# A graph layer on one core: other pacing of edge sums beside the residual loop, mixed rows three chunks ahead

## The chip, the core and the metric

The kernel runs on one core of a Trainium2 chip. A core has five engines, each with a program and a queue of its own: PE (matrix products and transposes, with weight loads shown as PEld), DVE (vector work), ACT (activations, copies, and issue of DMAs), POOL (elementwise work, and issue of gathers, that is, DMAs whose row numbers come from memory) and SP (issue of DMAs). 16 DMA engines carry all transfers. An engine works its instructions strictly in the order in which the program has them; one that waits for a semaphore holds up all behind it. The metric is the time of one execution in device microseconds (us), less is better. A measured time of a kernel here is the median of a few runs.

## What is computed

A layer of a graph transformer over 10,000 nodes with 512 features and 160,000 weighted edges, all in float32. Cut to what matters:

```
xn  = layernorm(x)
# graph part: messages along edges, summed at the edge's target (dst is sorted)
agg = segment_sum((xn @ W)[src] * edge_weight, dst);   gnn = relu(agg + bias)
# mixing part: attention that is linear in the nodes
q, k, v = heads(xn @ w_qkv.T);  q = softmax(q over 64 features);  k = softmax(k over nodes)
context = k.T @ v  (per head);  mix = layernorm(context applied to q, @ w_out.T) * gamma
x1  = x + gnn + mix
# feed-forward part: experts with weights chosen from the mean of layernorm(x1)
out = x1 + experts(layernorm(x1))
```

## The kernel before

**Tiling.** Rows are handled in 20 chunks: 19 of 512 nodes (128 partitions with four nodes each, SUB = 4) and a last one of 272. Features are four blocks of 128 (KB = 4). A product of 128 rows by 512 columns is four matmul calls in the source; the trace shows two passes for each, so "x8" in its rows is one such product.

**Edges.** `xn_d` holds the normalized rows in device memory. The edges stand in 1250 tiles of 128 edges. For each tile POOL gathers 128 rows of `xn_d` into a buffer `msg` (L556, 24 buffers in the pool `edge_m`, L826), DVE makes a selector `sel` of 128 x 32 (L562, L564), and PE multiplies (L574, the product `pm`): four tiles side by side fill the 128 output rows, one window of 32 rows each. Such a group of four tiles (eight up to tile 768, where two tiles share a window) is copied by ACT (L577, `part`) and written to `part_d` in device memory (L578). Where a target node's edges run over from one window to the next, the overlap is added by a carry: a DMA on POOL's queue that adds rows of `part_d` to others (L641). The matrix W is applied later, to the sums.

**The stages.** First rows are normalized and keys and queries are made (up to about 1070 us): queries are written to `qT_d`, and G gathers keys times rows. Then a data-dependent branch (L676 to L684, not taken here), then the small products that make the mixing matrix `mix` from G (L906 to L932). Then the residual loop (L1011 to L1063) makes x1 for each chunk, and the last stage (L1308 to L1332) applies the experts.

**The residual loop.** `attention(c)` (L986) loads the queries of a chunk (`qT`, one buffer) and its rows (`xt`, one buffer) on SP's queue, makes four products `po` with `mix`, and lets ACT and DVE turn them into `ot` (four buffers). It runs two chunks ahead of the loop: chunks 0 and 1 ahead of it (L1011), chunk c + 2 in round c. In round c the summed messages of the chunk's nodes, gathered by POOL from `part_d` into `at` (L963, two buffers, 1 MiB a chunk), are turned by 16 transposes into `aT` (`transposed`, L192, all copies on ACT), multiplied by `wg` (four products `pg`, L200) and added to `ot`, which SP writes to `x1_d` (L1032). The transposes and the next chunk's gather (`nodes_rows`, L1016) stand just ahead of the last of the four `po` products (L994).

**What sets the order.** PE's order is written out by hand (L903, `manual_schedule`): PE executes in the order of the Python calls. The order on the other engines is set by the compiler's scheduler from the same program. Edge groups are strewn among PE's other products by `work` (L664): each call reports estimated own work of PE in us (0.83 for each 128 x 512 matmul call, `PRODUCT`), the total is kept in `done[1]`, and edges are consumed up to tile `done[1] / PACE`, with PACE = 0.9. `edges_to` (L654) issues the gathers of a group when more than 16 tiles (AHEAD) are no longer in hand, so POOL's program runs 16 to 20 tiles ahead of PE's. A chunk's node gather may read only sums that are complete. The table AT_HAND (L35) says up to which window that must be for chunks below a number, and `far_enough` (L945) consumes all edges up to there, wherever PE's order stands, before the gather is issued:

```
for n, w in AT_HAND:
    if c < n:
        edges_to(min(NQ, past(w // GROUP, LAG + LEAD) + 1))
        return w * WIN
```

For the last two chunks it consumes all edges, adds the last carry, and the 17 DMAs that load the experts' weights (`experts_weights`, L284) follow on POOL's queue.

Of the kernel before, what the change touches and what calls it, by code (L numbers as in the profile page):

```python
# [9 lines left out]
F32 = mybir.dt.float32  # L10
# [20 lines left out]
KEPT = 2  # L31
PRODUCT = 0.83
PACE = 0.9

AT_HAND = [(5, 320), (7, 384), (8, 424), (9, 472), (10, 520), (11, 560), (12, 604), (13, 640), (14, 680), (15, 716), (16, 752),  # L35
           (17, 788), (18, 820)]
# [14 lines left out]
def gps_layer_kernel(  # L51
# [230 lines left out]
    held_w = {}  # L282

    def experts_weights():  # L284
        wp = held_w["pool"] = ctx.enter_context(tc.tile_pool(name="f_w", bufs=1, reuse_waits="tile"))
        w1_sb = held_w["w1"] = wp.tile([P, KB, NBASE * P], F32, name="w1_sb")
        w2_sb = held_w["w2"] = wp.tile([P, NBASE, D], F32, name="w2_sb")
        held_w["w1_sum"] = wp.tile([P, 4, KH, PAIRS * P], F32, name="w1_sum")
        b1_sb = held_w["b1"] = wp.tile([P, NF], F32, name="b1_sb")
        b2_sb = held_w["b2"] = wp.tile([NE, D], F32, name="b2_sb")  # L290
        held_w["b2_rows"] = wp.tile([P, D], F32, name="b2_b")
        rw_sb = held_w["router"] = wp.tile([P, KB, NP], F32, name="rw_sb")
        nc.scalar.dma_start(rw_sb, router_t.rearrange("(k p) d -> p k d", p=P))
        nc.scalar.dma_start(b1_sb[:, : NF - 1], b1_a)
        nc.scalar.dma_start(b1_sb[: fsz[-1], NF - 1 :], b1_b)
        nc.scalar.dma_start(b2_sb, b2)
        for j in range(KB):
            for g in range(P // SQ):
                nc.gpsimd.dma_start(w1_sb[g * SQ : (g + 1) * SQ, j, :], features(w1)[j, g, :, : NBASE * P])
        nc.gpsimd.dma_start(w2_sb, w2[: NBASE * P, :].rearrange("(f p) d -> p f d", p=P))  # L300
# [81 lines left out]
    with ExitStack() as ph:  # L382
# [266 lines left out]
            carried.append((past(end // GROUP, LAG), partial(carry, w, end)))  # L649

        done = [0, 0.0]
        EARLY_TOTAL = PRODUCT * KB * EARLY * 3 * KB

        def edges_to(stop):  # L654
# [9 lines left out]
        def work(us):  # L664

            done[1] += us
            if not pools:

                normal_rows(int(done[1] / EARLY_TOTAL * (NCH + 1)) + 2 - len(normal))
                return  # L670
            edges_to(groups_of(int(done[1] / PACE)))

        in_order = ph.enter_context(ExitStack())
        in_order.enter_context(tc.manual_schedule(engines={mybir.EngineType.PE}))
# [231 lines left out]
        with ExitStack() as pb:  # L906
            tmp = pb.enter_context(tc.tile_pool(name="c_tmp", bufs=1, side="right", reuse_waits="tile"))
            rk = small.tile([P, KB], F32, name="rk")
            nc.vector.reciprocal(rk, ksum)
            GT = tmp.tile([P, KB, D], F32, name="GT")  # L910
            transposed(GT, G, P, psum, "ps")
            edges_to(done[0] + 1)
            heads = tmp.tile([P, KB, P], F32, name="heads")
            nc.vector.memset(heads, 0.0)
            for cb in range(KB):
                pc = psum.tile([P, P], F32, name="pctx", tag="ps")
                for kb in range(KB):
                    nc.tensor.matmul(pc, GT[:, kb, cb * P : (cb + 1) * P],
                                     wv[:, kb, cb * P : (cb + 1) * P],
                                     start=kb == 0, stop=kb == KB - 1)  # L920
                for b in (0, HEAD):
                    blk = slice(b, b + HEAD)
                    nc.vector.tensor_scalar(heads[blk, cb, blk], pc[blk, blk],
                                            rk[blk, cb : cb + 1], QSCALE, op0=ALU.mult, op1=ALU.mult)
                edges_to(done[0] + 1)
                pt = psum.tile([P, P], F32, name="pht", tag="ps")
                nc.tensor.transpose(pt, heads[:, cb, :], ident)
                headsT = tmp.tile([P, P], F32, name="headsT", bufs=2)
                nc.vector.tensor_copy(headsT, pt)
                pm = psum.tile([P, D], F32, name="pmix", tag="ps")  # L930
                nc.tensor.matmul(pm, headsT, wo[:, cb, :], start=True, stop=True)
                nc.scalar.copy(mix[:, cb, :], pm)  # L932
        kv_ctx.close()

        done[1] = max(done[1], tiles_of(done[0])[0] * PACE)

# [20 lines left out]
        def gathered(c):  # L959
            r = chunks[c][1]  # L960
            n_rows = far_enough(c)
            at = io.tile([P, SUB, D], F32, name="at")
            nc.gpsimd.indirect_dma_start(  # L963
                out=at[:r].rearrange("p s d -> p (s d)"), out_offset=None, in_=by_four[: n_rows // SUB, :],
                in_offset=bass.IndirectOffsetOnAxis(ap=row_of[:r, c : c + 1], axis=0))
            if not pools and not held_w:
                experts_weights()
            return at

        def queries_in(c):  # L970
            qT = io.tile([P, KB, SUB * P], F32, name="qT", bufs=1)
            nc.sync.dma_start(qT[:, :, : SUB * chunks[c][1]], qT_d[c])
            return qT

# [11 lines left out]
        def attention(c, beside):  # L986
# [2 lines left out]
            r = chunks[c][1]  # L989
            qT = queries_in(c)  # L990
            xt = rows_again(c)
            ot = io.tile([P, SUB, D], F32, name="ot", bufs=4)
            for s in range(SUB):
                if s == SUB - 1:  # L994
                    beside()
# [12 lines left out]
                                               xt[:r, s, :], op0=ALU.mult, op1=ALU.add)  # L1008
            return ot

        mixed = [attention(c, lambda: None) for c in range(2)]  # L1011
        for c, (_, r) in enumerate(chunks):
            ot, at = mixed.pop(0), held["at"]
            aT = io.tile([P, KB, SUB * P], F32, name="aT", bufs=1)

            def nodes_rows():  # L1016
                transposed(aT, at, r, psum, "ps", by_act=range(KB))
                if c + 1 < NCH:
                    held["at"] = gathered(c + 1)

            if c + 2 < NCH:
                mixed.append(attention(c + 2, nodes_rows))
            else:
                nodes_rows()

            for s in range(SUB):
                po = psum.tile([P, D], F32, name="pg", tag="ps")
                times(po, aT, s, r, wg)
                put_out(KB * PRODUCT)
                nc.vector.tensor_tensor(po[:r, :], po[:r, :], bias_b[:r], ALU.add)  # L1030
                nc.vector.scalar_tensor_tensor(ot[:r, s, :], po[:r, :], 0.0, ot[:r, s, :], op0=ALU.max, op1=ALU.add)
            nc.sync.dma_start(x1_d[c], ot[:r])  # L1032
# [32 lines left out]
        query_ctx.close()  # L1065

    w1_sb, w1_sum = held_w["w1"], held_w["w1_sum"]
    wp, w2_sb, b1_sb, b2_sb, b2_b, rw_sb = (
        held_w[name] for name in ("pool", "w2", "b1", "b2", "b2_rows", "router"))
    last = wg  # L1070

    psum_r = ctx.enter_context(tc.tile_pool(name="r_ps", bufs=1, space=PSUM, reuse_waits="tile"))
    pmean = psum_r.tile([1, D], F32, name="pmean")


    pw = wp.tile([1, NE, NP], F32, name="pw")
    nc.gpsimd.memset(pw, 0.0)
    for i, parts in enumerate(PARTITIONS_OF_6):
        for j, part in enumerate(parts):
            nc.gpsimd.memset(pw[:, j, i : i + 1], part / 6)  # L1080
    iota = wp.tile([1, NP], F32, name="iota")
    nc.gpsimd.iota(iota, pattern=[[1, NP]], base=0, channel_multiplier=0,
                   allow_small_or_imprecise_dtypes=True)
    ones_row = wp.tile([1, P], F32, name="ones_row")
    nc.gpsimd.memset(ones_row, 1.0)

    owner = wp.tile([P, NF, NE], F32, name="owner")
    nc.gpsimd.memset(owner, 1.0)
    nc.gpsimd.affine_select(owner, owner, pattern=[[P, NF], [-F, NE]], compare_op=ALU.is_ge, fill=0.0,
                            base=0, channel_multiplier=1)  # L1090
    nc.gpsimd.affine_select(owner, owner, pattern=[[-P, NF], [F, NE]], compare_op=ALU.is_ge, fill=0.0,
                            base=F - 1, channel_multiplier=-1)
    mean = wp.tile([1, D], F32, name="mean")
    meanT = wp.tile([P, KB], F32, name="meanT")
    lm = wp.tile([1, 8], F32, name="lm")
    probs = wp.tile([1, NP], F32, name="probs")
    top = wp.tile([1, 2], F32, name="top")
    comb = wp.tile([1, NP], F32, name="comb")
    e_row = wp.tile([1, NE], F32, name="e_row")
    more = wp.tile([1, 1], F32, name="more")  # L1100
    n_more = wp.tile([1, 1], I32, name="n_more")
    e_col = wp.tile([NE, P], F32, name="e_col")
    scale = wp.tile([P, NF], F32, name="scale")

    def mean_row():
        r = chunks[-1][1]
# [3 lines left out]
        mean_ctx.close()  # L1110
        pr = psum_r.tile([P, D], F32, name="pr")
        nc.tensor.matmul(pr[0:1, 0:1], msum, ones, start=True, stop=True)
        shift = wp.tile([1, 1], F32, name="shift")
        nc.vector.tensor_copy(shift, pr[0:1, 0:1])
        nc.vector.tensor_scalar(mean, pmean, shift, 1.0 / N, op0=ALU.add, op1=ALU.mult)

# [6 lines left out]
    def weights_of_experts():  # L1123
# [10 lines left out]
        for k in range(2):  # L1134
            nc.vector.tensor_reduce(top[:, k : k + 1], rest, axis=AX.X, op=ALU.max)

            at = wp.tile([1, NP], F32, name=f"top_at{k}")
            nc.vector.tensor_scalar(at, rest, top[:, k : k + 1], -100.0, op0=ALU.is_equal, op1=ALU.mult)
            nc.vector.tensor_tensor(at, at, iota, ALU.add)
            first = wp.tile([1, 1], F32, name=f"first{k}")  # L1140
            nc.vector.tensor_reduce(first, at, axis=AX.X, op=ALU.min)
            hk = wp.tile([1, NP], F32, name=f"hot{k}")
            nc.vector.tensor_scalar(hk, at, first, None, op0=ALU.is_equal)
            hot.append(hk)
            if k == 0:
                rest = wp.tile([1, NP], F32, name="rest")
                nc.vector.scalar_tensor_tensor(rest, hk, -2.0, probs, op0=ALU.mult, op1=ALU.add)
        nc.vector.tensor_tensor(lm[:, 3:4], top[:, 0:1], top[:, 1:2], ALU.add)
        nc.vector.reciprocal(lm[:, 4:5], lm[:, 3:4])
# [158 lines left out]
    with tc.manual_schedule(engines={mybir.EngineType.PE}):  # L1308
# [2 lines left out]
            nc.sync.dma_start(xt[: chunks[c][1]], x1_d[c])  # L1311
            return xt

        st_all = wp.tile([P, P // SQ, NCH, SUB, 2], F32, name="st_all")

        def all_stats():
            for c0, c1 in ((0, NCH // 2), (NCH // 2, NCH - 1)):
# [93 lines left out]
```

## Time and profile before

| | |
|---|---|
| time, median of 3 runs | 3309.79 us (3303.76 to 3318.09) |
| the profiled execution | 3313.32 us, span 3311.6 us |
| mean granted TensorE clock | 0.989 |
| PE busy | 3206.1 us (97%) |
| POOL busy | 1387.6 us (42%), nearly all of it before 1900 us |
| moved by DMA | 654 MB, 491 MB read and 167 MB written in device memory |
| mixing matrix, from the branch to the first `po` | 1074 to 1117 us |
| residual loop, from the first `po` to the last `pg` | 1117 to 1937 us |
| turn of chunk 0's gathered nodes, of chunk 12's | 1189.3, 1667.9 us |
| last edge product ends | 1870.6 us |

The span is from the first to the last instruction of the profiled execution; the runs' times are taken around it. "Turn" is the first of the 16 transposes of a chunk's gathered nodes; it marks the chunk's place in the loop. A busy engine need not be a fast one: a matmul that has to wait for its operand inside a row of others is counted as busy here. In the tables of waits, an arrow `<-` names what ended the wait; "issue" means that nothing in the profile did.

### The profile page before, as it was taken

The page shows a single profiled execution, that of the slowest core. Times are in us where ns is not written, and L with a number is a line of the kernel's source. Part 1 is how long each engine was busy: PE and PEld are TensorE (multiplying, and loading weights), DVE is VectorE, ACT ScalarE, POOL GpSimd, SP SyncE. Part 2 cuts the span into 40 slices and gives each one's busy share as a digit, 9 for nine tenths or more (in the row PEclk, how much of TensorE's full clock was granted, in tenths as well). Part 3 has the DMA queues.
Part 4 walks back from the last instruction along what each step waited for, and adds up shares of the span by engine and source line. Part 5 has one row for each costly group of instructions (what it writes and reads, how often), then busy time and mean ns, then how long its engine had stood idle before and what let it go on. Part 6 is the DMA issues. An engine that isn't in the chain of part 4 may idle for free.

```text
span 3311.6 us, 36107 instructions
## 1 busy us (share of the span) xinstructions
PE 3206.1 (97%) x12779; PEld 1893.4 (57%) x12779; DVE 1773.9 (54%) x3935; ACT 822.0 (25%) x1664; POOL 1387.6 (42%) x1416
## 2 busy tenths in 40 slices
PE   6999999999999789999999989999999999999998
PEld 3444444444443233333333358888888888888886
DVE  7855556555553256565655666445544455445533
ACT  4422222222221112222222132222222222222211
POOL 6667777777777777777777400000000000000000
PEclk9999999999999999999999989999999999999999
DMA  8778888888878899999999822222121212122111
GB/s 320 286 254 267 273 281 290 283 260 278 277 243 278 295 318 353 340 351 345 341 339 340 246 96 60 56 67 74 51 64 51 89 51 64 51 78 63 52 39 40
DMA packets 216011, 654.39 MB, mean 198 GB/s; under 512 B 34405, under 2 KB 74341, under 8 KB 188107
## 3 DMA queue, kind: packets, MB, share of 16 engines
q0 software_dynamic: 105552, 360.05, 33.7%
q1 hardware_dynamic: 67800, 169.56, 15.5%
q10 hardware_dynamic: 42464, 122.32, 9.5%
q8 instruction: 105, 1.72, 0.2%
q14 instruction: 90, 0.74, 0.1%
HBM read 491.21 MB, written 166.63 MB: 199 GB/s over the span
## 4 chain that ended last, share of the span: by engine, by line
PE 88%; DMA 8%; DVE 2%; issue 1%; POOL 1%; ACT 0%; POOLq 0%; DVEq 0%; SPq 0%; ACTq 0%
PE px L234 15%; PE p L234 12%; PE pz L234 11%; PE py L234 10%; PE pm L574 9%; PE po L200 8%; PE pg L200 8%; PE pc L871 7%; DMA msg<-xn_d,src_sb 4%; PE pt L192 3%; PE ph L234 2%; PE pk L200 2%; DMA xn<-in_x 1%; DMA z_d<-xt 1%; DMA at<-part_d,row_of 1%
## 5 line engine op out<-in xcount | busy, mean ns | idle before, releaser
L556 POOL DMA_INDIRECT msg<-xn_d,src_sb x1250 | 1230.9, 985 | 425.2 <-issue 196.5
L574 PE MATMUL pm<-msg,sel 128*32 128x512 f32 x2504 | 372.6, 603 | 19.4 <-DMA msg<-xn_d,src_sb 17.6
L200 PE MATMUL po<-G,qT 128*128 128x512 f32 (+1 forms) x640 | 297.2, 610 | 18.3 <-DMA qT<-qT_d 18.3
L200 PE MATMUL pg<-wq,aT 128*128 128x512 f32 (+1 forms) x640 | 294.1, 606 | 0.0
L871 PE MATMUL pc<-xn,ek 128*128 128x512 f32 (+1 forms) x640 | 286.4, 596 | 0.7 <-DVE G L874 0.6
L577 ACT COPY part<-pm 128x512 f32<-128x512 f32 x217 | 126.9, 585 | 611.5 <-PE pm L574 603.4
L574 PEld LDWEIGHTS pm<-msg,sel 128*32 128x32 f32 x2504 | 69.1, 109 | 288.1 <-issue 186.3
L200 PEld LDWEIGHTS po<-G,qT 128*128 128x128 f32 (+1 forms) x640 | 116.3, 190 | 186.2 <-issue 162.6
L200 PEld LDWEIGHTS pg<-wq,aT 128*128 128x128 f32 (+1 forms) x640 | 115.5, 188 | 177.1 <-issue 162.2
L234 PE MATMUL px<-xnT,w_sb 128*128 128x256 f32 (+1 forms) x800 | 203.7, 377 | 11.3 <-DVE u L1228 11.1
L157 DVE BATCH_NORM_STATS2 st<-ot 128x6 f32<-128x512 f32 (+1 forms) x160 | 110.2, 689 | 190.8 <-ACT ot L1001 190.2
L871 PEld LDWEIGHTS pc<-xn,ek 128*128 128x128 f32 (+1 forms) x640 | 117.0, 190 | 142.1 <-issue 130.8
L234 PE MATMUL p<-kq_sum,xs_b 128*128 128x512 f32 (+1 forms) x408 | 189.5, 600 | 0.0
L234 PE MATMUL px<-w_sb,hh 128*128 128x256 f32 (+1 forms) x800 | 185.7, 379 | 0.0
L234 PE MATMUL py<-xs,w_sum 128*128 128x256 f32 (+1 forms) x800 | 185.0, 374 | 0.0
L234 PE MATMUL py<-w_sum,hh 128*128 128x256 f32 (+1 forms) x800 | 179.2, 379 | 0.0
L234 PEld LDWEIGHTS px<-xnT,w_sb 128*128 128x128 f32 x800 | 150.4, 191 | 32.7 <-DVE u L1228 13.1
L234 PEld LDWEIGHTS px<-w_sb,hh 128*128 128x128 f32 (+1 forms) x800 | 150.0, 188 | 22.7
L234 PEld LDWEIGHTS py<-w_sum,hh 128*128 128x128 f32 (+1 forms) x800 | 150.0, 188 | 22.7
L234 PEld LDWEIGHTS py<-xs,w_sum 128*128 128x128 f32 x800 | 149.4, 190 | 19.6
L345 ACT ACTIVATE xn<-xn,st_all 128x128 f32<-128x128 f32 x288 | 114.8, 481 | 99.8 <-DMA xn<-x_d 92.1
L234 PEld LDWEIGHTS p<-kq_sum,xs_b 128*128 128x128 f32 (+1 forms) x408 | 73.6, 187 | 109.7 <-issue 84.4
(299 smaller groups left out, 4649.8 us busy)
## 6 DMA issues: line engine op xcount, KB each, us to landing
part_d<-part ACTq DMA_DIRECT2D x217, 256.0 KB
msg<-xn_d,src_sb POOLq DMA_INDIRECT x1250
xn<-in_x SPq DMA_DIRECT2D x19, 1024.0 KB
xn_d<-xn ACTq DMA_DIRECT2D x19, 1024.0 KB
qT_d<-qT ACTq DMA_DIRECT2D x19, 1024.0 KB
qT<-qT_d SPq DMA_DIRECT2D x19, 1024.0 KB
xt<-in_x SPq DMA_DIRECT2D x19, 1024.0 KB
x_d<-ot SPq DMA_DIRECT2D x19, 1024.0 KB
```

The source lines that it names most:

```text
L157: nc.vector.bn_stats(st[:r, s, :], t[:r, s, :])
L192: nc.tensor.transpose(pt[:, s * r : (s + 1) * r], t[:r, s, kb * P : (kb + 1) * P], ident[:r, :r])
L200: nc.tensor.matmul(po[:r, :], t[:, kb, s * r : (s + 1) * r], w[:, kb, :], start=kb == 0, stop=kb == KB - 1)
L234: nc.tensor.matmul(o, lhs[j], rhs[j], start=start and j == 0, stop=stop and j == n - 1, skip_group_check=True)
L345: nc.scalar.activation(xn[:, s, b * P : (b + 1) * P], xn[:, s, b * P : (b + 1) * P], AF.Identity, bias=st[:, b, s, 0:1], scale=st[:, b, s, ...
L556: nc.gpsimd.indirect_dma_start(out=m[k], out_offset=None, in_=xn_d, in_offset=bass.IndirectOffsetOnAxis(ap=src_sb[:, t0 + k : t0 + k + 1], ...
L574: nc.tensor.matmul(pm[h * WIN : (h + 1) * WIN, :], sel[:, k, :], m[k] if k < len(m) else m[0], start=j == 0, stop=j == batch - 1, skip_gro ...
L577: nc.scalar.copy(part, pm)
L871: nc.tensor.matmul(pc, ek[:r, s, cb * P : (cb + 1) * P], xn[:r, s, :], start=s == 0, stop=s == SUB - 1)
```

## The change

Five things are changed:

- The mixing products stand in three rows of four, that is, in the order all `pctx`, then one edge group, then all transposes `pht`, then all `pmix`. Before, each of the four blocks had `pctx`, an edge group, `pht`, `pmix`. So one edge group stands there instead of four.
- In the residual loop the pace is ROW_PACE = 1.03 us of own work for each edge tile instead of 0.9, and the count starts at the tile reached then.
- `attention` runs three chunks ahead (MIXED = 3), with two `qT` buffers and five `ot` buffers instead of one and four.
- The node gather of the next chunk is issued behind the third of the four `pg` products, for chunks up to 16, instead of ahead of the last `po` product; there is one `at` buffer instead of two.
- The small tiles of the router lie in a pool of their own (`f_r`), which is opened after the residual loop.

AT_HAND, AHEAD, the 24 `msg` buffers and the last stage stay as they are. The diff, cut to its core (the many lines that only take `rp` for `wp` are left out):

```diff
 PACE = 0.9
+ROW_PACE = 1.03
+MIXED = 3
...
         done = [0, 0.0]
+        pace = [PACE]
...
-            edges_to(groups_of(int(done[1] / PACE)))
+            edges_to(groups_of(int(done[1] / pace[0])))
...
                                             rk[blk, cb : cb + 1], QSCALE, op0=ALU.mult, op1=ALU.mult)
-                edges_to(done[0] + 1)
+            edges_to(done[0] + 1)
+            headsT = tmp.tile([P, KB, P], F32, name="headsT")
+            for cb in range(KB):
                 pt = psum.tile([P, P], F32, name="pht", tag="ps")
                 nc.tensor.transpose(pt, heads[:, cb, :], ident)
-                headsT = tmp.tile([P, P], F32, name="headsT", bufs=2)
-                nc.vector.tensor_copy(headsT, pt)
+                nc.vector.tensor_copy(headsT[:, cb], pt)
+            for cb in range(KB):
                 pm = psum.tile([P, D], F32, name="pmix", tag="ps")
-                nc.tensor.matmul(pm, headsT, wo[:, cb, :], start=True, stop=True)
+                nc.tensor.matmul(pm, headsT[:, cb], wo[:, cb, :], start=True, stop=True)
                 nc.scalar.copy(mix[:, cb, :], pm)
...
-        done[1] = max(done[1], tiles_of(done[0])[0] * PACE)
+        pace[0] = ROW_PACE
+        done[1] = tiles_of(done[0])[0] * ROW_PACE
...
-            at = io.tile([P, SUB, D], F32, name="at")
+            at = io.tile([P, SUB, D], F32, name="at", bufs=1)
...
-            qT = io.tile([P, KB, SUB * P], F32, name="qT", bufs=1)
+            qT = io.tile([P, KB, SUB * P], F32, name="qT")
...
-            ot = io.tile([P, SUB, D], F32, name="ot", bufs=4)
+            ot = io.tile([P, SUB, D], F32, name="ot", bufs=MIXED + 2)
...
-        mixed = [attention(c, lambda: None) for c in range(2)]
+        mixed = [attention(c, lambda: None) for c in range(MIXED)]
...
                 transposed(aT, at, r, psum, "ps", by_act=range(KB))
-                if c + 1 < NCH:
+                if NCH > c + 1 >= NCH - MIXED:
                     held["at"] = gathered(c + 1)
...
-            if c + 2 < NCH:
-                mixed.append(attention(c + 2, nodes_rows))
+            if c + MIXED < NCH:
+                mixed.append(attention(c + MIXED, nodes_rows))
...
                 put_out(KB * PRODUCT)
+                if s == SUB // 2 and c + 1 < NCH - MIXED:
+                    held["at"] = gathered(c + 1)
...
+    rp = ctx.enter_context(tc.tile_pool(name="f_r", bufs=1, reuse_waits="tile"))
```

More of the change, by code (lines that the diff above doesn't have):

```diff
@@ L284, in experts_weights @@
     def experts_weights():
-        wp = held_w["pool"] = ctx.enter_context(tc.tile_pool(name="f_w", bufs=1, reuse_waits="tile"))
+        wp = ctx.enter_context(tc.tile_pool(name="f_w", bufs=1, reuse_waits="tile"))
         w1_sb = held_w["w1"] = wp.tile([P, KB, NBASE * P], F32, name="w1_sb")
@@ L1067, in gps_layer_kernel @@
     w1_sb, w1_sum = held_w["w1"], held_w["w1_sum"]
-    wp, w2_sb, b1_sb, b2_sb, b2_b, rw_sb = (
-        held_w[name] for name in ("pool", "w2", "b1", "b2", "b2_rows", "router"))
+    w2_sb, b1_sb, b2_sb, b2_b, rw_sb = (
+        held_w[name] for name in ("w2", "b1", "b2", "b2_rows", "router"))
     last = wg
+    rp = ctx.enter_context(tc.tile_pool(name="f_r", bufs=1, reuse_waits="tile"))
     psum_r = ctx.enter_context(tc.tile_pool(name="r_ps", bufs=1, space=PSUM, reuse_waits="tile"))
     pmean = psum_r.tile([1, D], F32, name="pmean")
-    pw = wp.tile([1, NE, NP], F32, name="pw")
+    pw = rp.tile([1, NE, NP], F32, name="pw")
     nc.gpsimd.memset(pw, 0.0)
@@ L1080, in gps_layer_kernel @@
             nc.gpsimd.memset(pw[:, j, i : i + 1], part / 6)
-    iota = wp.tile([1, NP], F32, name="iota")
+    iota = rp.tile([1, NP], F32, name="iota")
     nc.gpsimd.iota(iota, pattern=[[1, NP]], base=0, channel_multiplier=0,
                    allow_small_or_imprecise_dtypes=True)
-    ones_row = wp.tile([1, P], F32, name="ones_row")
+    ones_row = rp.tile([1, P], F32, name="ones_row")
     nc.gpsimd.memset(ones_row, 1.0)
-    owner = wp.tile([P, NF, NE], F32, name="owner")
+    owner = rp.tile([P, NF, NE], F32, name="owner")
     nc.gpsimd.memset(owner, 1.0)
@@ L1092, in gps_layer_kernel @@
                             base=F - 1, channel_multiplier=-1)
[L1093 to L1103, printed above, removed]
+    mean = rp.tile([1, D], F32, name="mean")
+    meanT = rp.tile([P, KB], F32, name="meanT")
+    lm = rp.tile([1, 8], F32, name="lm")
+    probs = rp.tile([1, NP], F32, name="probs")
+    top = rp.tile([1, 2], F32, name="top")
+    comb = rp.tile([1, NP], F32, name="comb")
+    e_row = rp.tile([1, NE], F32, name="e_row")
+    more = rp.tile([1, 1], F32, name="more")
+    n_more = rp.tile([1, 1], I32, name="n_more")
+    e_col = rp.tile([NE, P], F32, name="e_col")
+    scale = rp.tile([P, NF], F32, name="scale")
     def mean_row():
@@ L1112, in mean_row @@
         nc.tensor.matmul(pr[0:1, 0:1], msum, ones, start=True, stop=True)
-        shift = wp.tile([1, 1], F32, name="shift")
+        shift = rp.tile([1, 1], F32, name="shift")
         nc.vector.tensor_copy(shift, pr[0:1, 0:1])
@@ L1135, in weights_of_experts @@
             nc.vector.tensor_reduce(top[:, k : k + 1], rest, axis=AX.X, op=ALU.max)
-            at = wp.tile([1, NP], F32, name=f"top_at{k}")
+            at = rp.tile([1, NP], F32, name=f"top_at{k}")
             nc.vector.tensor_scalar(at, rest, top[:, k : k + 1], -100.0, op0=ALU.is_equal, op1=ALU.mult)
             nc.vector.tensor_tensor(at, at, iota, ALU.add)
-            first = wp.tile([1, 1], F32, name=f"first{k}")
+            first = rp.tile([1, 1], F32, name=f"first{k}")
             nc.vector.tensor_reduce(first, at, axis=AX.X, op=ALU.min)
-            hk = wp.tile([1, NP], F32, name=f"hot{k}")
+            hk = rp.tile([1, NP], F32, name=f"hot{k}")
             nc.vector.tensor_scalar(hk, at, first, None, op0=ALU.is_equal)
@@ L1145, in weights_of_experts @@
             if k == 0:
-                rest = wp.tile([1, NP], F32, name="rest")
+                rest = rp.tile([1, NP], F32, name="rest")
                 nc.vector.scalar_tensor_tensor(rest, hk, -2.0, probs, op0=ALU.mult, op1=ALU.add)
@@ L1312, in residual_rows @@
             return xt
-        st_all = wp.tile([P, P // SQ, NCH, SUB, 2], F32, name="st_all")
+        st_all = rp.tile([P, P // SQ, NCH, SUB, 2], F32, name="st_all")
         def all_stats():
```

## The prediction

> **What bounds the kernel now.** I read the page's busy shares and chain first, then the table of stretches, PE's waits, PE's time line, and POOL's groups. PE leads the page:
>
> ```profile
> PE 3206.1 (97%) x12779; PEld 1893.4 (57%) x12779; DVE 1773.9 (54%) x3935; ACT 822.0 (25%) x1664; POOL 1387.6 (42%) x1416
> ```
>
> 97% is an average over stages. The change sits between about 1074 us (products that make the mixing matrix) and 1937 us (first product of the last stage). In that stretch (columns: PE, PEld, DVE, ACT, POOL busy with counts, PE clock, DMA share, GB/s):
>
> ```profile
> 1118.00:1190.00 72.00, 53.70 (x173) 20.42 (x172) 26.81 (x60) 10.96 (x20) 52.36 (x53) 0.86 0.84 290
> 1190.00:1300.00 110.00, 110.00 (x402) 42.07 (x400) 71.00 (x186) 25.43 (x50) 80.16 (x82) 1.00 0.97 353
> ...
> 1600.00:1700.00 100.00, 99.97 (x353) 36.32 (x352) 63.58 (x166) 21.46 (x41) 77.14 (x78) 1.00 0.97 348
> ```
>
> PE looks full from 1190 on, but so do the DMA engines (0.97), and POOL's 77% is full as well, as its own groups between 1100 and 1850 us show:
>
> ```profile
> L556 POOL DMA_INDIRECT msg<-xn_d,src_sb x536 | 532.3, 993 | 182.5 <-issue 93.6 <-DMA msg<-xn_d,src_sb 35.1 <-PE pm L574 24.6
> L963 POOL DMA_INDIRECT at<-part_d,row_of x18 | 17.1, 948 | 7.5 <-issue 3.7 <-DMA part_d<-part_d 2.3 <-DMA msg<-xn_d,src_sb 0.9
> L641 POOL DMA_DIRECT2D part_d<-part_d x12 | 11.7, 974 | 0.0
> ```
>
> 566 issues in 750 us are 1.325 us each; nearly every idle gap is the same 0.30 us, so 0.95 + 0.30 = 1.25 us is the floor and about 1.30 the working rate. PE's waits:
>
> ```profile
> PE po L200 <- DMA qT<-qT_d: 18.3, 2, 9.2
> PE pm L574 <- DMA msg<-xn_d,src_sb: 17.6, 22, 1.8
> ...
> PE pt L192 <- DMA at<-part_d,row_of: 6.0, 1, 6.0
> ```
>
> The msg line understates: a pm row's duration holds waits of the tiles in it. A row of 8 takes 1.00 us unhindered (4 edge tiles, two passes). From 1300 to 1882 us the pm rows hold 812 matmuls, 101.5 us at that rate, and last 143: **42 us of starvation hidden in busy time**. So this stretch is bound by POOL's gathers, with PE close behind. The last pm ends at 1870.6 us.
>
> **What the change removes.** PE's time line:
>
> ```profile
> 1129.49 3.70 PE L200 MATMUL po<-G,qT 128*128 128x512 f32 x8
> 1142.41 6.08 PE L200 MATMUL po<-G,qT 128*128 128x512 f32 x8 [9.21 <-DMA qT<-qT_d]
> ...
> 1171.99 6.65 PE L200 MATMUL po<-G,qT 128*128 128x512 f32 x8 [9.09 <-DMA qT<-qT_d]
> ```
>
> A second qT buffer lets the 9 us load run beside a whole chunk's products: 18.3 us go, and with them the slow clock behind each wait (6.08 and 6.65 against 3.70): 5.3. Together 23.6 us.
>
> The mixing products take 1074.1 to 1117.3, 43.2 us, because four 8-tile edge groups stand among them while POOL restarts after the branch of L682. The changed order has one group there besides the one before: 3.65 (transposes, slow clock) + 2 x 1.9 (groups) + 4.2 (pctx) + 0.6 (one headsT wait) + 1.3 (pht) + 4.4 (pmix) = 18.0. That is 25.2 us less on PE, three groups of it only postponed (5.7 us).
>
> First turn of gathered nodes: now at 1189.3; minus 25.2, minus 23.6, plus the third chunk's four products ahead (14.5), plus 8 tiles that come later (1.9) = 1157 us, with 744 tiles consumed instead of 760.
>
> **The pace.** In the changed kernel's built order the 12 chunks that follow consume 744 to 1052 tiles, 25.7 each (now 29.3). PE per chunk: 8 products of 3.63 + 1.85 (turn) + 25.7 x 0.25 = 37.3 us; POOL: 25.7 x 1.30 + 1.3 (node gather) + 0.9 (carry) = 35.6 us. No starvation; chunk 12's turn comes at 1157 + 12 x 37.3 = 1604 us. Now it comes at 1667.9, with 1112 tiles done. So 64 us are won, and 60 tiles (60 x 1.30 = 78 us of POOL) are owed.
>
> **Where they fall due.** The due table AT_HAND is unchanged: a node gather still first consumes all edges up to its window. From chunk 12 on the order is
>
> ```
> pt at x16, po x4, pg x12, pm x36, pg x4, po x12, pt at x16, ...
> ```
>
> (before: pm x4 after each product, never more), and POOL's order puts each node gather behind the 16 look-ahead tiles of the next burst. With 24 msg buffers and one at buffer this is a loop, from one node gather's issue to the next:
> - its landing: not shown alone. The least lead an at had without PE waiting is 13.0 us (chunk 18); a msg with a quarter of its bytes waited for with little else moving took 3.74; the msg tiles that starve PE under load had 7.2 to 7.6. I take 7.5, nearest the loaded rows; ends 3.7 and 13.
> - the turn 1.9, plus slow clock behind a wait of some 11 us: 2.4 (as above; ends 0 and 2.95).
> - po x4, pg x12: 14.5. Meanwhile POOL fills its buffers (8 more tiles, 10 us) and rests.
> - the burst frees buffers: 36 + 16 - 24 = 28 msgs at 1.30, a carry and the gather, 1.3 each: 39.0.
>
> Sum **65.3 us** against 40.5 for a chunk now. ACT's copies and DVE's selectors are 9 a burst at 0.6 to 0.7 us each, hidden in it.
>
> The way to the last pm: chunk 12's turn to 13's: 18.4 of products and 8 tiles, then 24 msgs, carry and gather (33.8) and the landing = 60. Three loops to chunk 16: 196. Chunk 16 has its burst directly behind its turn: 4.3 + 33.8 + 7.5 = 46. Then chunk 17's turn and 20 tiles already landed: 7. 1604 + 60 + 196 + 46 + 7 = 1913, against 1870.6: **42 us later**. Behind the last pm the chain is the same in both (sum written, carry, node gather, weights, last node gather, which PE reaches 48 us after the last pm now, waiting 6.0): chunk 18's turn loses its cover, chunk 17's pg alone (14 us against 26), but the wait only moves ahead of the later one. The last stage's products and their order do not change: 0.
>
> Other edits. Node gathers into one buffer instead of two: in chunks 1 to 11 they issue 20 us or more before their turn, hidden; from 12 on it is the loop above. Five ot and two qT: SP issues qT ahead of xt, 9 us loads in a 37 us chunk, 0. Router tiles in a pool of their own, opened after the stage: POOL's small memsets are queued behind the last node gather in either kernel, 0; if they waited for freed space until the last pg, a few us.
>
> On one term a page speaks. The trace's node gather is bounded by 3.7 and 13 us. The Trainium skill, DMA: Bandwidth & Descriptors, "Anatomy of one DMA — SWDGE (gpsimd) path", fits 2.0 us plus bytes over 436 GB/s, which for 1 MiB makes an estimate of 4.4 us; its 2.6 for a msg is below the 3.74 measured here. By it the loop would be 62.2 and the end 15 us earlier than my sum.
>
> **Sum.** The profiled execution took 3313.3 us (span 3311.6 and 1.7 around it); plus 42 is 3355. The median of the three runs, 3309.8, is 3.5 lower: forecast 3351, +1.3%.
> Low end (landing 3.7, no slow clock, 1.25 per msg): loop 57.6, the other pieces 55, 38 and 7, last pm 1877, +6: 3316. High end (13, 2.95, 1.325): loop 72, pieces 66, 52 and 9, last pm 1947, +76: 3386.
>
> **Rivals.**
> - *POOL never rests (faster).* If the look-ahead kept POOL issuing through the products, 571 issues from 1099 at 1.29 end at 1836 instead of 1858, 22 us earlier, and the early 43 us on PE are kept as far as that: 3288. It decides where PE reaches each burst before the 24 buffers are full, in under 10 us after the gather instead of 24. For it: POOL's 1.25 us floor. Against: 14.5 us of products stand before each burst. Chance 0.06.
> - *The loop is short (no change).* Node gathers land like a msg on idle queues, since bursts leave the DMA engines gaps: the low end, 3316. For it: 3.74 us. Against: the burst itself is when POOL's queue is full. Chance 0.14.
> - *The single at buffer binds everywhere.* If a node gather needs the 20.7 us of the last one, behind the weights, the loop grows by 13, five times: 3416. Against: nothing that large is queued there. Chance 0.08.
> - Forecast: 0.72. That the change doesn't reach the order is excluded: the built order shows it.
>
> About 0.5%, 16 us, is what a measurement can tell from no change. The forecast's and the last rival's cases lie above it (0.80), the short loop within (0.14), the first rival below (0.06). 3316 to 3386 leaves out the first and third rival and a little beyond: 2 in 10.
>
> **What would show it.** Right: no wait on qT; chunk 12's turn near 1604; from then on PE waits for at, some 10 us a chunk, three to six times, pm rows of 72 matmuls lasting over 15 us, POOL idle over 10 us a chunk, turns 60 to 68 us apart; the last stage as long as now. Wrong: turns under 45 us apart after chunk 12, no wait on at, or starved pm before it.

## The result and the profile after

The changed kernel takes 3357.64 us (median of 4 runs, 3355.74 to 3358.06), the kernel before 3310.14 us beside it (4 runs, 3303.76 to 3318.09). The ratio is 1.0142, 95% interval 1.0128 to 1.0157: slower, 47.5 us between the medians. The profiled execution took 3357.8 us with a span of 3356.1 and a mean granted clock of 0.979.

The page's first part after the change, in the order PE, PEld, DVE, ACT, POOL:

```profile
PE 3199.8 (95%) x12779; PEld 1907.2 (57%) x12779; DVE 1783.6 (53%) x3935; ACT 823.2 (25%) x1664; POOL 1384.3 (41%) x1416
```

The same instructions, PE 6 us less busy, and the span 44 us longer: the loss is idle PE. Where it lies, the table of stretches after the change shows (columns as in the prediction):

```profile
1118.00:1190.00 72.00, 72.00 (x260) 28.76 (x258) 45.33 (x107) 13.91 (x27) 53.32 (x55) 1.00 0.96 353
1190.00:1300.00 110.00, 110.00 (x395) 42.92 (x392) 71.89 (x185) 25.29 (x49) 80.75 (x83) 1.00 0.97 352
1600.00:1700.00 100.00, 80.87 (x255) 26.55 (x254) 42.31 (x109) 16.44 (x30) 66.15 (x68) 0.93 0.84 285
1700.00:1800.00 100.00, 73.51 (x215) 30.52 (x213) 37.74 (x94) 15.68 (x29) 60.12 (x62) 0.86 0.77 249
```

The first row is the gain: PE is now full from 1118 on (before 53.70 of 72). The last two rows are the loss: from 1600 on PE, POOL, the DMA engines and the clock all fall together (from 1600 to 1700 us POOL is busy for 66.15 us with 68 instructions instead of 77.14 with 78). So no single one of them is the bound here; the time lines below show them waiting for each other in turn. PE's waits over the whole execution:

```profile
PE pt L194 <- DMA at<-part_d,row_of: 67.9, 7, 11.6
PE pm L576 <- DMA msg<-xn_d,src_sb: 19.7, 28, 2.1
...
PE pm L576 <- ACT part L579: 6.1, 5, 1.9
...
PE po L202 <- DMA qT<-qT_d: 2.2, 1, 2.2
```

In these lines the numbers are the total in us, the number of waits and the longest. The wait on qT went from 18.3 to 2.2 us, and a wait on the node gathers came, 67.9 us in seven waits where there was one of 6.0. One turn of that loop in PE's time line after the change:

```profile
1663.89 3.68 PE L194 MATMUL pt<-ident,at 128*128 128x128 f32 x16 [9.48 <-DMA at<-part_d,row_of]
1667.36 3.71 PE L202 MATMUL po<-G,qT 128*128 128x512 f32 x8
1670.90 10.46 PE L202 MATMUL pg<-wq,aT 128*128 128x512 f32 x24
1681.30 5.81 PE L576 MATMUL pm<-msg,sel 128*32 128x512 f32 x48
...
1701.70 3.70 PE L202 MATMUL pg<-wq,aT 128*128 128x512 f32 x8
1705.24 10.46 PE L202 MATMUL po<-G,qT 128*128 128x512 f32 x24
1726.57 3.68 PE L194 MATMUL pt<-ident,at 128*128 128x128 f32 x16 [10.86 <-DMA at<-part_d,row_of]
```

The 36 tiles come in one burst, from 1681.30 to 1701.70: 20.4 us for 9 us of work. The first 24 tiles, whose buffers were full, run in 5.81 us (48 matmuls); the other twelve are waited for. Behind the burst stand 14 us of products and then a wait of 10.86 us for the next node gather. POOL's time line over the same turn:

```profile
1657.89 0.94 POOL L969 DMA_INDIRECT at<-part_d,row_of  x1 [0.31 <-DMA msg<-xn_d,src_sb]
1659.14 0.94 POOL L558 DMA_INDIRECT msg<-xn_d,src_sb  x1 [0.30 <-issue]
...
1667.89 0.95 POOL L558 DMA_INDIRECT msg<-xn_d,src_sb  x1 [0.30 <-PE pt L194]
1682.62 0.94 POOL L558 DMA_INDIRECT msg<-xn_d,src_sb  x1 [13.78 <-PE pm L576]
```

Behind the node gather POOL issues eight messages, all 24 buffers are taken, and it rests 13.78 us until the burst's first `pm` gives one back. The engine that set the pace before has been made to rest once a chunk. Its groups between 1100 and 1850 us after the change:

```profile
L558 POOL DMA_INDIRECT msg<-xn_d,src_sb x503 | 497.1, 988 | 213.5 <-issue 82.1 <-PE pm L576 66.3 <-DMA msg<-xn_d,src_sb 38.3
```

503 messages instead of 536, and 66.3 us of rest ended by PE's `pm` instead of 24.6. These 41.7 us more of rest are where the time goes: the last message is issued at 1894.4 us instead of 1857.5, 36.9 later.

### The profile page after: what moved, and what is told of

It is laid out like the page before. It is cut to its first block, busy times and chain, and to the rows that moved or that the text cites. A ratio compares the mean times of both kernels' runs of the same rounds, so it can differ in the third digit from the quotient of the medians.

```text
span 3356.1 us, 36107 instructions
## 1 busy us (share of the span) xinstructions
PE 3199.8 (95%) x12779; PEld 1907.2 (57%) x12779; DVE 1783.6 (53%) x3935; ACT 823.2 (25%) x1664; POOL 1384.3 (41%) x1416
## 4 chain that ended last, share of the span: by engine, by line
PE 59%; DMA 7%; issue 1%; POOL 1%; DVE 1%; ACT 0%; POOLq 0%; DVEq 0%; SPq 0%; ACTq 0%
PE px L236 15%; PE pz L236 11%; PE py L236 10%; PE po L202 8%; PE pg L202 8%; PE pm L576 4%; DMA msg<-xn_d,src_sb 3%; PE ph L236 2%; DMA at<-part_d,row_of 2%; PE pt L194 1%; DMA z_d<-xt 1%; DMA xt<-x_d 1%; POOL msg L558 1%; DMA x_d<-ot 0%; DMA qT<-qT_d 0%
## 5 line engine op out<-in xcount | busy, mean ns | idle before, releaser
L576 PE MATMUL pm<-msg,sel 128*32 128x512 f32 x2504 | 359.7, 604 | 26.2 <-DMA msg<-xn_d,src_sb 19.7
L202 PE MATMUL po<-G,qT 128*128 128x512 f32 (+1 forms) x640 | 289.5, 602 | 2.2 <-DMA qT<-qT_d 2.2
L564 DVE TENSOR_TENSOR sel<-iota_w,place 128x128 f32<-128x128 f32 (+2 forms) x217 | 74.4, 343 | 140.4 <-PE pm L576 140.4
```

The costliest lines, as they stand in the source:

```text
L202: nc.tensor.matmul(po[:r, :], t[:, kb, s * r : (s + 1) * r], w[:, kb, :], start=kb == 0, stop=kb == KB - 1)
L564: nc.vector.tensor_tensor(sel[:, :n], iota_w[:, None, :].to_broadcast([P, n, WIN]), place[:, t0 : t0 + n, None].to_broadcast([P, n, WIN]), ...
L576: nc.tensor.matmul(pm[h * WIN : (h + 1) * WIN, :], sel[:, k, :], m[k] if k < len(m) else m[0], start=j == 0, stop=j == batch - 1, skip_gro ...
```

## The experiments

The theory: the loss is the tiles that the pace owes, taken in bursts, together with a node gather whose place in POOL's queue is behind the look-ahead of the next burst; from the start of a burst to the next node gather POOL has 36 + 16 messages less its buffers to issue, and once its buffers are full it rests through the products. Rivals: the three chunks of mixed queries or the single `at` buffer cost the time by themselves; or the node gather's landing alone sets the loop. Each ratio is against runs of the kernel before on the same chip: median 3313.97 us for the first four runs below, 3311.08 for the mixing rows alone, for pace 0.95 and for the first two with the early last gather, 3312.48 for those with other `msg` buffers.

### Undoing one part at a time

**Pace 0.9 in the changed kernel.**

```diff
-ROW_PACE = 1.03
+ROW_PACE = 0.9
```

> The changed kernel with the old pace in the residual loop (0.9 for 1.03), nothing else. Theory: the loss is made by edges that are owed and fall due in bursts, each with a node gather behind 16 look-ahead tiles. At 0.9 the built order has no burst above 12 tiles, and only before the last two chunks, so waits on at go but for those at the end, POOL issues without rest and sets the pace as it did before the change: last edge product 1860 to 1870 us (before 1870.6, changed 1907.7), time 3303 to 3312. Rival 'place': the late node gather into one buffer costs at any pace: PE waits for at in most chunks, time above 3340. Rival 'three ahead': more traffic ahead of the loop is what costs: above 3340 too, with longer waits for msg from the first chunks on.

Measured: 3311.55 us, ratio 0.9989 (0.9977 to 1.0001), last pm at 1865.3. One constant takes the whole loss away; three chunks ahead, one `at` buffer, the later gather and the router's pool stay, and together they cost nothing that can be seen at this pace. The table of stretches of this run, and its wait on node gathers:

```profile
1700.00:1800.00 100.00, 98.49 (x340) 35.54 (x338) 59.91 (x156) 21.43 (x42) 75.84 (x78) 1.00 0.95 326
```

```profile
PE pt L194 <- DMA at<-part_d,row_of: 20.6, 3, 13.1
```

PE and POOL are full again in a stretch where the changed kernel has 73.51 and 60.12 us busy; of the waits only the last three chunks' are left. But what PE wins early (chunk 0's turn at 1160.9 instead of 1189.3, with the products of one chunk more, 14.5 us, done by then) doesn't show either: 1160.9 to 1658.6 takes 12 chunks of 41.5 us, which is POOL's pace (30 tiles a chunk at 1.30 us, a node gather and a carry).

**Pace 1.03 alone, in the kernel before.**

```diff
+        pace = [PACE]
...
-            edges_to(groups_of(int(done[1] / PACE)))
+            edges_to(groups_of(int(done[1] / pace[0])))
...
-        done[1] = max(done[1], tiles_of(done[0])[0] * PACE)
+        pace[0] = 1.03
+        done[1] = tiles_of(done[0])[0] * 1.03
```

> The kernel before with the pace 1.03 in the residual loop alone. Theory (bursts times place): the built order has the same bursts of 28 to 36 tiles from chunk 12 on, but the node gather stands ahead of the last po product, so 5 products and 3 more (some 28 us) lie between a burst and the turn that needs the gather, and only the POOL-limited burst itself is paid: last edge product 1880 to 1895, time 3320 to 3335. Rival 'pace alone': late edges are the whole loss whatever the place: 3350 to 3365. Rival 'place alone': no change, 3305 to 3315.

Measured: 3335.25 us, ratio 1.0060 (1.0041 to 1.0079), last pm at 1887.0. From chunk 12 on the turns stand 50 to 51 us apart instead of 64, and PE hardly waits for node gathers there: with the gather ahead of the last `po`, the burst still starves PE (1676.8 to 1698.5, 21.7 us for 36 tiles), but the gather, issued at 1714.8, lands under the products behind the burst (1698.5 to 1726.1). So the pace alone costs about 21 us (the time is at the upper end of the range expected), and the rest of the 47.5 needs something beside it.

**The node gather at its old place, in the changed kernel** (the pace stays 1.03, and there is still one `at` buffer).

```diff
-                if NCH > c + 1 >= NCH - MIXED:
+                if c + 1 < NCH:
                     held["at"] = gathered(c + 1)
...
-                if s == SUB // 2 and c + 1 < NCH - MIXED:
-                    held["at"] = gathered(c + 1)
```

> The changed kernel with the node gather issued where it stood before (ahead of the last po product), one at buffer and the pace 1.03 kept. Theory: bursts stay as long as in the changed kernel, but po x4, pg x16 and po x12 now cover the gather and POOL's look-ahead, so waits on at in chunks 13 to 16 fall from some 10 us to 0 to 3 and turns stand 45 to 50 us apart there instead of 63 to 69: last edge product 1870 to 1885, time 3313 to 3328. Rival 'pace alone': no change against the changed kernel, 3350 to 3365. Rival 'one at buffer': at waits stay, above 3340.

Measured: 3325.19 us, ratio 1.0033 (1.0021 to 1.0046), last pm at 1878.9; turns 56, 49.9, 51.8, 54.8 us apart, where 45 to 50 were expected; PE waits 2.4 us at most before a turn up to chunk 16, and only 0.3 of that is put down to `at`. Some 36 us of the loss are gone with the place, and one buffer is no burden: this speaks against the rival of the single buffer.

**Look-ahead 8 instead of 16 in the residual loop of the changed kernel.**

```diff
+        ahead = [AHEAD]
...
-                while sum(len(m) for _, m, _ in held["edges"]) <= AHEAD and i + len(held["edges"]) < NQ:
+                while sum(len(m) for _, m, _ in held["edges"]) <= ahead[0] and i + len(held["edges"]) < NQ:
...
         pace[0] = ROW_PACE
+        ahead[0] = 8
```

> The changed kernel with 8 instead of 16 tiles of look-ahead in the residual loop (AHEAD itself stays 16 up to there). It changes the one term of the predicted loop in which the node gather queues on POOL behind the next burst's first tiles: 36 + 8 - 24 = 20 msgs instead of 28. Theory: the gather issues some 10 us earlier in each round, the waits on at of 10.8 us in chunks 13 to 16 go to about 0 to 2, turns 50 to 55 us apart: last edge product 1868 to 1882, time 3312 to 3328. Rival 'burst': the burst itself, limited by POOL's rate, is the loss and less look-ahead starves PE more: 3355 or above. Rival 'landing': the gather is slow to land for want of DMA bandwidth, not late to issue: leads of 7 us grow, no gain, 3350 to 3360.

Measured: 3326.33 us, ratio 1.0031 (1.0019 to 1.0042), last pm at 1880.9; turns 53.4, 53.3, 52.2 apart. The gather's place among PE's products is unchanged; it has only 8 messages fewer ahead of it in POOL's queue, which the formula prices at 8 x 1.30 = 10.4 us a loop. Measured: 64.0 less 53.0, the means of three loops, 11.0.

**The mixing rows alone, in the kernel before.**

```diff
-                edges_to(done[0] + 1)
+            edges_to(done[0] + 1)
+            headsT = tmp.tile([P, KB, P], F32, name="headsT")
+            for cb in range(KB):
...
+            for cb in range(KB):
                 pm = psum.tile([P, D], F32, name="pmix", tag="ps")
```

> The kernel before with the mixing products in three rows of four alone (one edge group among them instead of four; pace 0.9, two chunks ahead, old place of the gather, two at buffers). Theory: POOL's gathers bound this stretch, so the 20 us and more that PE wins there are not kept. The 24 postponed tiles are never paid back by the pace, since its count is started at the tile reached; they fall due in bursts of 16 to 24 tiles from chunk 14 on. First turn some 20 us earlier, last edge product 1870 to 1888, time 3312 to 3330. Rival 'PE's time is kept': first turn 20 us earlier and everything behind it too, 3288 to 3296.

Measured: 3323.73 us, ratio 1.0053 (1.0034 to 1.0073). Chunk 0's turn comes 25.6 us earlier (1163.7), the last pm 6.9 us later (1877.6). 25 us saved on PE bring nothing, as POOL's last message goes out at 1860.2 instead of 1857.5. Its wait on node gathers:

```profile
PE pt L192 <- DMA at<-part_d,row_of: 17.7, 3, 14.7
```

The last gather alone grows from 6.0 to 14.7. The last turn, chunk 19's, comes 8.4 us later (1927.3 instead of 1918.9). Why this is slower by more than POOL's 2.7 us is not settled: the last chunks, whose gathers now have a lead of 13 to 14 instead of 36 to 53 us, are where it shows.

**Pace 0.95 in the changed kernel** (as the first, with 0.95).

> The changed kernel with the pace 0.95. Theory: between the two paces the bursts shrink (up to 16 tiles before chunk 15, 24 and 32 behind it), POOL rests little; waits on at before chunks 17 to 19 only, and perhaps 16. Last edge product 1860 to 1872, time 3305 to 3318, the same as at 0.9 within the noise. Rival 'every tile owed costs': half way between the pace 0.9 and the changed kernel, 3330 to 3340.

Measured: 3313.87 us, ratio 1.0011 (0.9999 to 1.0023). One loop (61.7 us from chunk 15's turn to chunk 16's) is left where 1.03 has four (68.6, 62.7, 64.6 and 64.8), and the time is 0.2% above that of pace 0.9 by the two ratios, some 7 us, with intervals that just overlap. So the loss does not grow evenly with every tile owed, as the rival had it (3330 to 3340); that it goes by the number of loops fits, but rests on this one loop.

### Changing the size of the loop

PE's order is the same to the instruction in these two; only the buffers of `msg` change.

```diff
-                pools["m"] = edge_ctx.enter_context(tc.tile_pool(name="edge_m", bufs=24,
+                pools["m"] = edge_ctx.enter_context(tc.tile_pool(name="edge_m", bufs=27,
```

> The changed kernel with 27 msg buffers instead of 24; PE's order is the same. By the loop of the prediction the messages between two node gathers are 36 + 16 less the buffers: 25 instead of 28, so 3 x 1.30 = 3.9 us less in each of five pieces from chunk 12's turn on: last pm near 1888 (1907.7 with 24), turns of chunks 13 to 16 some 61 us apart instead of 64, time 3338 (3332 to 3344). Rival (the node gather's landing and its wait set the loop, and POOL's rest costs nothing): no change, 3354 to 3360, turns still 63 to 65 apart.

> The changed kernel with 20 msg buffers instead of 24; PE's order is the same. By the loop: 32 messages between two node gathers, 4 x 1.30 = 5.2 us more in each of five pieces: last pm near 1934, turns of chunks 13 to 16 some 70 us apart, time 3384 (3374 to 3396, the upper part if chunks before 12 now starve as well). Rival (landing sets the loop): 3354 to 3362, turns still 63 to 65 apart.

Measured: 3345.36 us with 27 buffers (ratio 1.0100, 1.0085 to 1.0114), 3386.49 us with 20 (1.0222, 1.0207 to 1.0237). The turns from chunk 13 to 16 are 59.2 and 68.6 us apart on average, against 64.0 with 24: 4.8 less and 4.6 more, expected 3.9 and 5.2. From chunk 11's turn to the last pm it is 330.6, 348.6 and 376.5 us with 27, 24 and 20: 18.0 less and 27.9 more, expected 19.5 and 26. The pieces were expected from chunk 12's turn on, and from there it is 17.5 less and 13.9 more: with 20 buffers the other 14 us are lost one chunk earlier (50.2 us from chunk 11's turn to 12's instead of 36.2). The time with 27 is 1.4 us above its range: its first `po` came at 1096.8 us instead of 1091.0, having waited 7.4 us for qT instead of 2.2. What makes that wait longer is not known. POOL's messages between 1100 and 1850 us, first with 27 buffers, then with 20:

```profile
L558 POOL DMA_INDIRECT msg<-xn_d,src_sb x511 | 503.9, 986 | 205.2 <-issue 84.8 <-PE pm L576 50.3 <-DMA msg<-xn_d,src_sb 33.6
```

```profile
L558 POOL DMA_INDIRECT msg<-xn_d,src_sb x490 | 486.6, 993 | 225.6 <-PE pm L576 83.1 <-issue 81.1 <-DMA msg<-xn_d,src_sb 39.0
```

The rest that `pm` ends is 50.3, 66.3 and 83.1 us: every buffer is worth rest on POOL. From chunk 13 to 17 the gathers' lead, from issue to turn, is 6.0 to 7.5 us in all three, so the rival of the landing alone falls: it is a term of the loop and does not set its change.

### A version a little faster than both

**Pace 0.9, and the last chunk's node gather ahead of the weights' loads**, into a free `qT` buffer. In both kernels that gather stands behind 17 loads of weights in POOL's queue.

```diff
-            at = io.tile([P, SUB, D], F32, name="at", bufs=1)
+            at = io.tile([P, SUB, D], F32, name="at", **(dict(tag="qT") if c == NCH - 1 else dict(bufs=1)))
...
-            if not pools and not held_w:
+            if c == NCH - 1:
                 experts_weights()
...
+                if c + 1 == NCH - 1:
+                    held["at"] = held.pop("last")
+                elif NCH > c + 1 >= NCH - MIXED:
                     held["at"] = gathered(c + 1)
+                    if c + 1 == NCH - 2:
+                        held["last"] = gathered(NCH - 1)
```

> The changed kernel with pace 0.9 and the last chunk's node gather issued right behind that of the last but one, into a free qT buffer, ahead of the 16 remaining loads of the experts' weights instead of behind them. Theory: the last gather's lead of 20 us is the weights' DMAs ahead of it in its queue; moved, it lands within some 9 us, the wait before the last turn (13.1 us at 0.9) goes, and the last stage starts 9 to 13 us earlier after the last edge product: time 3294 to 3304. Rival 'weights are due': the first products of the last stage then wait for the weights instead, and nothing is won, 3306 to 3314.

Measured: 3305.82 us, ratio 0.9988 (0.9977 to 0.9999): between the range expected and the rival's. PE's waits in this run:

```profile
PE pt L194 <- DMA at<-part_d,row_of: 9.8, 2, 9.5
...
PE pg L202 <- ACT aT L196: 6.0, 1, 6.0
```

The last chunk's wait (13.1 us with pace 0.9 alone) is gone; 9.5 us of wait for chunk 18's gather and 6.0 us for ACT's copies of `aT` stand in its place. The last stage begins at 1925.4 instead of 1933.6, but of these 8 us only 3 are in the time (5.3 us under the kernel before by the medians, against 2.4 with pace 0.9 alone). The profiled execution, 3310.5 us, is one of the longer of its twelve, and its last stage took 1383.4 us instead of the 1376.4 of the run with pace 0.9 alone; why it did stays open, and with it where the other 5 us went.

**The same with pace 0.95.**

> As the run before, with pace 0.95. Theory: 3294 to 3306, within 5 us of the pace 0.9. Rival 'weights are due': 3306 to 3318.

Measured: 3312.78 us, ratio 1.0005 (0.9994 to 1.0016). That misses the range expected. It lies in the rival's, but not for the rival's reason: in the profiled execution the first product of the last stage waits 0.9 us, for DVE's `w_sum`, as it does with pace 0.9. The loop from chunk 15 to 16 is there (62.8 us), as with pace 0.95 alone; that it makes the 7 us more than with pace 0.9 is argued, not shown.

**Pace 0.9, the early last gather, and 27 buffers.**

> Row pace 0.9 and the last chunk's node gather ahead of the weights' loads, with 27 msg buffers instead of 24. The bursts are small at this pace, so 3 more buffers smooth single starved groups only: 3300 to 3307, last pm 1852 to 1859. Rival (POOL's rate alone binds at this pace): as with 24 buffers, 3304 to 3308, last pm 1858 to 1862.

Measured: 3301.96 us (6 runs, 3299.7 to 3311.29), ratio 0.9969 (0.9957 to 0.9981): the fastest here, 10.5 us (0.3%) under the kernel before by the medians and 56 under the changed kernel, within the range expected. The execution that was profiled is the longest of the six (3311.3 us, last pm at 1862.7), so its trace does not show where the 5 us more than with 24 buffers come from; that stays open.

Not tried: two `qT` buffers, three chunks ahead or the router's own pool by itself in the kernel before; so the wait on qT was not removed by itself.

## Why the prediction was right

Forecast 3351, measured 3357.6. By its steps:

| step | predicted | measured |
|---|---|---|
| mixing products to the first `po` | 18.0 | 18.4 (1072.62 to 1091.01) |
| chunk 0's turn | 1157 | 1154.8 |
| a chunk, up to chunk 12 | 37.3 | 36.7 |
| chunk 12's turn | 1604 | 1595.3 |
| from there to chunk 13's | 60 | 68.6 |
| three loops | 65.3 each | 62.7, 64.6, 64.8 |
| chunk 16 to 17 | 46 | 43.2 |
| last pm | 1913 (+42) | 1907.7 (+37.0) |
| from last pm to the last stage | as before, 66 | 68.8 (+2.7) |
| last stage | as before | +4.7 |
| profiled execution | 3355 | 3357.8 |

- **The mixing products and qT** were right. PE's time line after the change shows the rows of four:

```profile
1072.62 3.65 PE L194 MATMUL pt<-ident,G 128*128 128x128 f32 x16 [7.25 <-DVEq L685]
1076.19 2.33 PE L576 MATMUL pm<-msg,sel 128*32 128x512 f32 x16
1078.45 3.84 PE L921 MATMUL pctx<-wvo,GT 128*128 128x128 f32 x32
...
1091.01 10.54 PE L202 MATMUL po<-G,qT 128*128 128x512 f32 x24 [2.21 <-DMA qT<-qT_d]
```

One short wait on qT stays, at the first product of all, where the prediction said none.

- **The loop** is right in its mechanism and within 1 to 3 us in size, and the runs with other buffers, look-ahead and place move it as its formula says. Its terms: the node gather's lead was 6.0 to 7.5 us where PE waited for it in chunks 13 to 17, against 7.5 taken and ends of 3.7 and 13. The estimate of 4.4 us by the fit in the Trainium skill, DMA: Bandwidth & Descriptors, "Anatomy of one DMA — SWDGE (gpsimd) path", is below every one of them; the measurement decides. From the burst's first `pm` to the next gather's issue it was 37.9, 38.8 and 38.7 us, against 39.0. The slow clock is there in every loop: the transposes behind the wait took 3.68 us instead of 1.91, and the `po` after them 3.71, 4.79 and 4.91 instead of 3.60, so 1.9, 3.0 and 3.1 us instead of 2.4. Before chunk 12 the gathers had leads of 16 to 27 us instead of 20 or more, and were hidden as said.
- **Mis-sized: the piece after chunk 12's turn**, 68.6 instead of 60. The step took the 24 buffers as full before the burst, with 24 messages left to issue. At 1595.3 PE had used 1052 tiles and POOL had issued 1061, nine ahead. At the eleven turns before it was 12 to 16 ahead, so the buffers were not full there either, and ahead of chunk 12's own gather POOL idled for 8.33 us at 1574 to 1583, some six messages. From 1595.3 to the next gather POOL has 47 messages and a carry to issue without rest, 62.6 us or 1.30 each, and the gather's lead is 6.0. The 8.6 us missing here and the 8.7 won before chunk 12 cancel by luck, so that the last pm came within 6 us.
- **Mis-sized: what lies behind the last pm**, costed at nothing and measured at 7.4 us. Behind the last pm the turns of chunks 18 and 19 wait for their gathers now (9.2 and 10.5 us, before only the last, 6.0), and the last stage took 1379.5 us instead of 1374.8. The latter is no effect of the change that a run isolates: in the other runs that keep the changed last chunks it took 1376.3 to 1382.6, and in the two that keep the old ones (pace alone, rows alone) 1378.0 and 1376.4.
- **The rivals.** POOL does rest (13.8 to 16.3 us a loop); the loop is not short; the single buffer does not bind where the bursts are small (pace 0.9) or the gather stands earlier. The question that the prediction answered by a sum, whether 64 us won early are kept, the runs answer too: with pace 0.9 next to nothing is owed and next to nothing is kept (the last message goes out at 1855.4 us instead of 1857.5), for POOL sets the end in both.

## What to carry to other kernels

Where one engine feeds another through a few buffers, work that the consumer puts off is not saved but comes back in a burst, and the feeder can prepare no more of it than its buffers hold: count burst plus look-ahead less buffers at the feeder's rate, and add what stands in its queue behind them. A gather's place in the source is not its place in its queue; one that is issued "later" stands behind all that the look-ahead puts before it, and is free only while its lead exceeds its landing. Time won on an engine that is 97% busy can be worth nothing where its busy rows hide waits for another, as the 28 us that chunk 0's turn came earlier with pace 0.9; look at what the other engine's idle time is ended by.

## What the runs showed of the hardware

- POOL was idle for 8.33 us ahead of chunk 12's node gather, right behind a carry issued at 1573.73. The profile names no releaser; that the gather waits for the carry to land would explain it, and is argued, not shown. In the kernel before, the profile puts the 2.28 us ahead of chunk 15's gather down to the carry (`DMA part_d<-part_d`), with pace 0.95 the 4.34 us ahead of chunk 14's.
- Three buffers for sums on their way out (`part`) are felt in bursts: with bursts of 36 tiles ACT's copies wait 21.2 us for the writes of earlier sums and PE 6.1 us for ACT; with pace 0.9 it is 1.7 us, and no wait of PE.
- The granted clock is lower where PE idles: 0.86 from 1700 to 1800 us in the changed kernel, with PE busy for 73.51 us, and 1.00 in the run with pace 0.9 in the same stretch, with 98.49.
